# Gate and up with the weights stationary and two token tiles moving, and VectorE's 32x32 turns around the quantisations

## The chip, the core and the metric

The kernel runs on one core of one Trainium2 chip. The metric is the device time of one execution in microseconds. Before the change it is 4258.46 us, the median of three runs (4257.51 to 4258.61). Engine names: TensorE (PE, with its weight loads PEld), VectorE (DVE), ScalarE (ACT), GpSimd (POOL) and SyncE (SP, which issues the DMAs here).

## The reference

One transformer block on x of 8 x 1024 x 512, all in float32. The normed x goes into a causal attention of 16 heads and into a gated network whose linear layers are quantised to a four-bit grid in blocks of 16 along the contracted dimension. Cut to what matters:

```python
def fp4_quant_dequant(x):                       # blocks of 16 along the last dim
    xb = x.reshape(shape[:-1] + (shape[-1] // 16, 16))
    scale = maximum(max(abs(xb), -1, keepdims=True) / 6.0, 1e-12)
    xn = xb / scale
    return (_GRID[searchsorted(_MID, abs(xn))] * sign(xn) * scale).reshape(shape)

def fp4_linear(x, w):                           # w is (n, k)
    return einsum('bsk,nk->bsn', fp4_quant_dequant(x), fp4_quant_dequant(w))

xn = layernorm(x)
h = silu(fp4_linear(xn, w_gate)) * fp4_linear(xn, w_up)      # 512 -> 1408
out = x + attention(xn) + fp4_linear(h, w_down)              # 1408 -> 512
```

## The kernel before

The 8192 tokens are 64 tiles of 128. Attention runs in 64 units (8 batches, 8 pairs of heads). The work is written as generators, and `merge` (L1010) interleaves them into one order of instructions per engine. Each step says its cost on TensorE, the earliest time at which its inputs are there, and how many PSUM banks it needs. A model of time (`clock`, with `act`, `dve` and `pool` for the other engines, L145 to L161) decides which stream goes next, and `Later` (L163) puts an action off to a due time. That order is fixed when the program is built: each engine runs its own queue in order, SP's too.

The streams, each with a place per tile: `weigh` (the softmax weights and their product with the values, L682), `maxima` (row maxima and sums, L557), `networks` (the gated network, L785), `quantised` (x for the network, L438), `preparations` (norm, transpose, projections to q, k and v, 16 tiles ahead, L412) and `finish` (the output projection and the sum, L914).

PSUM has eight banks here: six in a shared set (`Banks`, L187), one accumulator `acc` for the down product, and one, `y`, for the attention. `take` hands out the bank that comes free first, and `back` says when.

The network's way for one tile of 128 tokens:

- `normed` (L392) norms the tokens in `xt`; its `apply` writes them to `xn_kept` in HBM (L408). `quantised` reads them back into `xs` (L442), quantises them on VectorE (`Quantised`, L267, whose operations are L335 to L344) and has TensorE transpose them (`transposed`, L347: four transposes into a bank at L351, one ScalarE copy at L352) into `xqT`.
- `product` (L824) computes gate, later up, for a chunk of 512, 512 or 384 hidden features: `xqT` is the stationary operand, 128 features by 128 tokens, and the weights `wgT` or `wuT` move (L831). The result lies in a bank with tokens on the partitions.
- `gated` (L841) applies SiLU on ScalarE into `hid`, `hidden` (L847) multiplies by up on VectorE, and `Quantised` quantises `hid` in place along its columns, which are the features.
- `turn` (L788) has TensorE transpose the quantised `hid` into a bank, and ScalarE copies it to `hqT`; `down` (L794) multiplies `hqT` by `wdT` (L809) into `acc`. After the last chunk VectorE adds the residual (L815), and the sum goes to `part_kept` in HBM.

Chunks are taken in pairs (L861): both gate products, the down product of the first older chunk, both up products with the transposes of the older second chunk between, its down product, and then the transposes of this pair's first chunk. At most two quantisations run at once; a third forces the rest of the first one out at once (L280).

`project` (L453) computes q and k in another form: the weights `wa` are stationary and two tiles, 256 tokens of `xnT`, move (L466).

Of the kernel before, what the change touches and what calls it, by code (L numbers as in the profile page):

```python
# [27 lines left out]
def kernel(  # L28
# [61 lines left out]
    CW = 4 * P  # L90
    chunks = [(c, min(CW, I - c)) for c in range(0, I, CW)]

# [94 lines left out]
    class Banks:  # L187


        def __init__(self):  # L190
            self.tiles = [ps_g.tile([P, W], F32, name=f"bank{k}") for k in range(6)]
            self.at = [0.0] * 6
            self.held = set()
# [73 lines left out]
    class Quantised:  # L267
# [10 lines left out]

        def __init__(self, src, w, xs, after=0.0):
            while len(running) > 1:  # L280
                running[0].done()
            running.append(self)
            self.out, self.end = xs, 0.0
            self.left = []
            start = max(0.0, after - clock[0])
            for wide, us, engine, action in self.operations(src, w, xs):
                us = us + wide * w / CW
                self.left.append(Later(start, lambda us=us, engine=engine, action=action: self.one(us, engine, action)))
                start += SPREAD * us
            self.expected = clock[0] + start  # L290
# [66 lines left out]
    def weights_quantised():  # L357
# [7 lines left out]
        def load(src, dst, r, c, w):  # L365
            raw = p3.tile([P, CW], F32, name="hid")[:, :w]
            nc.sync.dma_start(out=raw, in_=src[r : r + P, c : c + w])
            return raw
# [23 lines left out]
    def normed(tl):  # L392

        xt = tl.xt
        stats = p4.tile([P, 6], F32, name="stats")
        mv = p4.tile([P, 2], F32, name="mv")
        rstd = p4.tile([P, 1], F32, name="rstd")
        nc.vector.bn_stats(stats, xt)
        nc.vector.bn_aggr(mv, stats)
        nc.vector.tensor_scalar_add(rstd, mv[:, 1:2], EPS)  # L400
        nc.gpsimd.tensor_tensor(rstd, rstd, power, ALU.pow)
        end = pool(0.6, dve(1.1))

        def apply():
            nc.vector.tensor_scalar(xt, xt, mv[:, 0:1], rstd, ALU.subtract, ALU.mult)
            tl.ready = dve(0.57)
            tl.xn = dram.tile([P, D], F32, name="xn_kept", bufs=AHEAD + LAG + 4)
            tl.kept = Later(tl.ready - clock[0] + 0.5, lambda: nc.sync.dma_start(out=tl.xn, in_=xt))  # L408

        tl.applied = Later(end - clock[0] + HOP, apply)  # L410

    def prepare(n):  # L412
# [6 lines left out]
        for i, tl in enumerate(pair):  # L419
            while tl.applied is None:  # L420
                yield 0.0, clock[0] + 0.5, 0
            tl.applied.now()
            yield 0.0, tl.ready, 1
            end = transposed(xnT[:, :, i * P : (i + 1) * P], tl.xt, NC)
            yield 0.45, 0.0, 0
            tl.kept.now()
        for i, tl in enumerate(tiles[n + QT : n + 2 * QT]):
# [9 lines left out]

    def quantised(tl):  # L438

        tl.kept.now()  # L440
        xs = p1.tile([P, CW], F32, name="xs")
        nc.sync.dma_start(out=xs, in_=tl.xn)  # L442
        yield 0.0, clock[0] + 5.0, 0
        xq = Quantised(xs, D, xs)
        yield from xq.wait()
        xqT = p3.tile([P, NC, P], F32, name="xqT")
        tl.there = transposed(xqT, xq.done(), NC)
        tl.xqT = xqT
        yield 0.45, 0.0, 0

# [333 lines left out]

    def network(tiles):  # L785
        emptied = [0.0]

        def turn(job):  # L788
            yield from job.hq.wait()
            job.hqT = p2.tile([P, CW // P, P], F32, name="hqT")  # L790
            job.turned = transposed(job.hqT[:, : job.w // P, :], job.hq.done(), job.w // P)
            yield 0.11 * job.w / P, 0.0, 0

        def down(job):  # L794
            tl = job.tl
            yield 0.0, max(job.turned, emptied[0] if job.i0 == 0 else 0.0), 0
            if job.i0 == 0:
                tl.acc = ps_a.tile([P, D], F32, name="acc")
                tl.xr = p3.tile([P, D], F32, name="res")
                nc.sync.dma_start(out=tl.xr, in_=x[tl.b, tl.t * P : (tl.t + 1) * P, :])  # L800

                def with_bias():
                    nc.gpsimd.tensor_tensor(tl.xr, tl.xr, bp, ALU.add)
                    pool(1.35)

                tl.biased = Later(6.0, with_bias)
            for j in range(job.w // P):
                i = job.i0 // P + j
                nc.tensor.matmul(  # L809
                    tl.acc, lhsT=job.hqT[:, j, :], rhs=wdT[:, i, :], start=(i == 0), stop=(i == NI - 1)  # L810
                )
                if i == NI - 1:
                    xr = tl.xr
                    tl.biased.now()
                    nc.vector.tensor_tensor(xr, tl.acc, xr, ALU.add)  # L815
                    emptied[0] = dve(0.7, clock[0] + 0.86)
                    tl.part = dram.tile([P, D], F32, name="part_kept", bufs=NT + 10)
                    tl.stored = Later(
                        emptied[0] - clock[0] + 1.0, lambda: nc.sync.dma_start(out=tl.part, in_=xr)
                    )  # L820
                if j % 2 == 1 or j == job.w // P - 1:
                    yield 0.86 * (j % 2 + 1), 0.0, 0

        def product(job, wT):  # L824
            while job.tl.xqT is None:
                yield 0.0, clock[0] + 1.0, 0
            yield 0.0, job.tl.there, 1
            job.bank, g = banks.take()
            job.g = g[:, : job.w]
            for c in range(NC):  # L830
                nc.tensor.matmul(  # L831
                    job.g,
                    lhsT=job.tl.xqT[:, c, :],
                    rhs=wT[:, c, job.i0 : job.i0 + job.w],
                    start=(c == 0),
                    stop=(c == NC - 1),
                )
                if c == 1:
                    yield 1.72 * job.w / CW, 0.0, 0

        def gated(job):  # L841
            job.hid = p3.tile([P, CW], F32, name="hid")[:, : job.w]
            nc.scalar.activation(job.hid, job.g, AF.Silu)  # L843
            job.gated = act(job.w, clock[0] + 1.72 * job.w / CW, "silu")
            banks.back(job.bank, job.gated)

        def hidden(job):  # L847
            nc.vector.tensor_tensor(job.hid, job.hid, job.g, ALU.mult)  # L848
            end = dve(0.7, max(job.gated, clock[0] + 1.72 * job.w / CW))
            banks.back(job.bank, end)  # L850
            job.hq = Quantised(job.hid, job.w, job.hid, end)

        def jobs():
            for tl in tiles:
                for i0, w in chunks:
                    yield Job(tl, i0, w)

        stream = jobs()
        older = []
        while True:  # L860
# [3 lines left out]
            for job in pair:  # L864
                yield from product(job, wgT)
                if job is pair[-1]:
                    for each in pair:
                        gated(each)
                yield 1.72 * job.w / CW, 0.0, 0
            if older:  # L870
                yield from down(older[0])
            for k, job in enumerate(pair):
                yield from product(job, wuT)
                hidden(job)
                yield 1.72 * job.w / CW, 0.0, 0
                if k == 0 and older[1:]:
                    yield from turn(older[1])
            if older[1:]:
                if not pair:
                    yield from turn(older[1])  # L880
                yield from down(older[1])
            if pair:
                yield from turn(pair[0])
            older = pair
# [3 lines left out]
    def fetch(tl):  # L888
# [8 lines left out]
        else:  # L897
            parts = [p1.tile([P, NC, P], F32, name=f"yT{part}") for part in range(2)]
            inv = p1.tile([P, NC, P], F32, name="inv_y")
            part = p3.tile([P, D], F32, name="res")  # L900
        for k, yT in enumerate(parts):
# [60 lines left out]
    class Job:  # L962
        def __init__(self, tl, i0, w):
            self.tl, self.i0, self.w = tl, i0, w

    class Tile:
        def __init__(self, n):
            self.n, self.b, self.t = n, n // NT, n % NT
            self.part, self.stored, self.xqT, self.applied, self.fetched = None, None, None, None, None

# [81 lines left out]
    EARLY = PIECES - 6  # L1052
    tiles = [Tile(n) for n in range(N)]
    units = [Unit(n) for n in range(N)]
    batches = []
    units_begun = [-1]

    with tc.manual_schedule(
# [40 lines left out]
        load_values(units[0])  # L1099
        net = network(tiles)  # L1100
        TILE = sum(4 * 1.72 * w / CW + w / P * 0.97 for _, w in chunks)

# [27 lines left out]
        def preparations():  # L1130
            for n in range(AHEAD, N, QT):
# [7 lines left out]
                Stream(networks()),  # L1139
                Stream((quantised(tl), 0.45, tl.n + LAG - 1, 0.5) for tl in tiles),  # L1140
                Stream(preparations()),
# [41 lines left out]
```

## Time and profile before

| What | Value |
|---|---|
| median of three runs | 4258.46 us |
| span of the profiled execution, first to last instruction | 4249.7 us |
| TensorE busy | 4131.2 us (97%), 17684 instructions |
| its weight loads busy | 2619.1 us (62%) |
| VectorE, ScalarE, GpSimd busy | 2763.2 (65%), 2321.8 (55%), 546.5 us (13%) |
| DMA | 573.84 MB, mean 135 GB/s |
| gate and up on TensorE (L831) | 676.1 and 662.9 us busy, 1536 instructions each |
| down (L809) | 665.4 us busy, 1408 instructions |
| transposes (L351) | 836 of hid, 256 of xs, 256 of xt |
| copies of transposed tiles on ScalarE (L352) | 199.0 us busy |
| VectorE in 0 to 500, 2000 to 2500, 3600 to 3900 us | 356.0, 316.9, 209.0 us |

The profiled execution's own time is its span and what lies around it; the median is 8.8 us above the span. Busy time is the union of an engine's instructions. Matmuls overlap in a pipeline and their ends are modelled, so TensorE's busy share is not a measure of its rate. In the waits view each row names who waited, for whom, the sum, how often and the longest.

### The profile page before, as it was taken

How to read it: one execution, taken by the hardware profiler on the slowest of the kernel's cores; microseconds unless marked ns; L12 is line 12 of the kernel's file. 1: busy time of each engine (PE TensorE's matmuls, PEld its weight loads, DVE VectorE, ACT ScalarE, POOL GpSimd, SP SyncE). 2: the span in 40 equal slices, each digit the busy share in tenths (PEclk: the TensorE clock that was granted, in tenths of full speed). 3: DMA queues.
4: the chain of work that ended last, by engine and by line, in shares of the span. 5: the costliest groups of instructions: out<-in, count | busy, mean ns of one | idle time of the engine just before them, and what ended most of it. 6: DMA issues, size and time to landing. Idle time of an engine off the chain costs nothing.

```text
span 4249.7 us, 58555 instructions
## 1 busy us (share of the span) xinstructions
PE 4131.2 (97%) x17684; PEld 2619.1 (62%) x17684; DVE 2763.2 (65%) x7323; ACT 2321.8 (55%) x5918; POOL 546.5 (13%) x1296
## 2 busy tenths in 40 slices
PE   7789999999999999999999999999999999999998
PEld 6666666666666666666666666666666555555555
DVE  6786765666575666575666575666565666667755
ACT  2246556565555565555565555565555666666640
POOL 0001111111111111111111111111111111111110
PEclk9889999999999999999999999999999999999999
DMA  5654434455455455455455455455454433333314
GB/s 183 177 173 129 124 103 120 118 157 157 132 155 150 140 164 153 132 156 151 140 160 155 134 154 149 141 162 153 138 149 131 117 92 94 95 92 93 93 56 126
DMA packets 564187, 573.84 MB, mean 135 GB/s; under 512 B 114976, under 2 KB 420128, under 8 KB 563872
## 3 DMA queue, kind: packets, MB, share of 16 engines
q1 hardware_dynamic: 563872, 570.10, 48.3%
q8 instruction: 142, 2.33, 0.2%
q14 instruction: 173, 1.42, 0.1%
HBM read 400.56 MB, written 169.35 MB: 134 GB/s over the span
## 4 chain that ended last, share of the span: by engine, by line
PE 82%; ACT 7%; DVE 4%; DMA 1%; issue 1%; SPq 0%; ACTq 0%; POOL 0%; DVEq 0%
PE bank L831 26%; PE acc L809 12%; PE bank L466 8%; PE y L706 7%; PE bank L724 6%; PE bank L727 6%; PE bank L597 5%; PE bank L936 5%; PE bank L511 4%; ACT bank L568 3%; PE bank L351 2%; ACT L568 1%; ACT L843 1%; ACT pr L735 1%; DMA ks<-y_kept 1%
## 5 line engine op out<-in xcount | busy, mean ns | idle before, releaser
L568 ACT ACTIVATE bank<-bank,neg 128x512 f32<-128x512 f32 (+3 forms) x1536 | 856.7, 559 | 163.7 <-DVE neg L610 119.8
L735 ACT ACTIVATE pr<-bank 128x512 f32<-128x512 f32 (+3 forms) x1536 | 662.7, 494 | 482.6 <-PE bank L727 478.2
L741 POOL TENSOR_SCALAR_AFFINE_SELECT pr<-pr 128x128 f32<-128x128 f32 x1024 | 393.2, 397 | 3238.3 <-ACT pr L735 3228.9
L610 DVE CUSTOM_DVE_ANT_0 bank<-bank,mask 128x128 f32<-128x128 f32 (+3 forms) x1024 | 501.2, 500 | 469.5 <-PE bank L597 455.7
L724 PE MATMUL bank<-shT,pick 128*128 128x512 f32 (+3 forms) x1536 | 683.8, 453 | 2.7 <-DVE hid L848 1.5
L831 PE MATMUL bank<-wuT,xqT 128*128 128x512 f32 (+1 forms) x1536 | 676.1, 565 | 3.9 <-ACT bank L568 1.0
L809 PE MATMUL acc<-wdT,hqT 128*128 128x512 f32 x1408 | 665.4, 596 | 1.3 <-ACT hqT L352 1.3
L831 PE MATMUL bank<-wgT,xqT 128*128 128x512 f32 (+1 forms) x1536 | 662.9, 561 | 0.0
L597 PE MATMUL bank<-ks,qs 128*128 128x512 f32 (+3 forms) x1536 | 636.2, 475 | 24.7 <-ACT bank L568 21.7
L727 PE MATMUL bank<-qs,ks 128*128 128x512 f32 (+3 forms) x1536 | 516.9, 346 | 0.0
L622 DVE TENSOR_REDUCE neg<-bank 128x1 f32<-128x512 f32 x512 | 345.7, 685 | 186.8 <-PE bank L597 185.6
L597 PEld LDWEIGHTS bank<-ks,qs 128*128 128x128 f32 x1536 | 277.5, 191 | 234.1 <-issue 111.3
L831 PEld LDWEIGHTS bank<-wuT,xqT 128*128 128x128 f32 x1536 | 277.0, 190 | 228.8 <-issue 158.9
L831 PEld LDWEIGHTS bank<-wgT,xqT 128*128 128x128 f32 x1536 | 280.0, 190 | 219.3 <-issue 151.9
L724 PEld LDWEIGHTS bank<-shT,pick 128*128 128x128 f32 x1536 | 290.4, 189 | 155.7 <-issue 78.9
L809 PEld LDWEIGHTS acc<-wdT,hqT 128*128 128x128 f32 x1408 | 255.3, 190 | 197.0 <-issue 183.6
L478 ACT ACTIVATE full<-bank,bqk 128x256 f32<-128x256 f32 x256 | 107.4, 470 | 491.1 <-PE bank L466 409.3
L727 PEld LDWEIGHTS bank<-qs,ks 128*128 128x128 f32 x1536 | 290.6, 189 | 110.6 <-issue 77.1
L466 PE MATMUL bank<-xnT,wa 128*128 128x256 f32 x1536 | 349.8, 381 | 0.9 <-ACT xnT L352 0.6
L466 PEld LDWEIGHTS bank<-xnT,wa 128*128 128x128 f32 x1536 | 288.4, 190 | 55.6 <-issue 18.9
L706 PE MATMUL y<-pr,vs 128*32 128x512 f32 (+3 forms) x3072 | 316.5, 501 | 0.8 <-POOL pr L741 0.8
L568 ACT ACTIVATION_READ_ACCUMULATOR bank<-bank,neg 128x1 f32 x1536 | 315.4, 205 | 0.0
(99 smaller groups left out, 4674.7 us busy)
## 6 DMA issues: line engine op xcount, KB each, us to landing
wa<-in_L_attn_W_attn_dram SPq DMA_DIRECT2D x146, 512.0 KB
qs<-qk_kept SPq DMA_DIRECT2D x512, 128.0 KB
ks<-qk_kept SPq DMA_DIRECT2D x512, 128.0 KB
wp<-in_L_attn_W_proj_dram SPq DMA_DIRECT2D x81, 512.0 KB
qk_kept<-high SPq DMA_DIRECT2D x128, 256.0 KB
qk_kept<-full SPq DMA_DIRECT2D x128, 256.0 KB
y_kept<-yu SPq DMA_DIRECT2D x256, 128.0 KB
yT<-y_kept SPq DMA_DIRECT2D x112, 256.0 KB
```

Of the source, the lines that this page charges most:

```text
L466: nc.tensor.matmul(pq[:, j, :], lhsT=halves[j][:, c, :], rhs=xnT[:, c, :], start=(c == 0), stop=(c == NC - 1),)
L568: nc.scalar.activation(part, part, AF.Exp, bias=neg[:, kind, k + j : k + j + 1], scale=1.0 if kind == 1 else -1.0, accum_out=sums[:, kind, ...
L597: nc.tensor.matmul(sc[:, j * n : (j + 1) * n], lhsT=un.qs[Q][:, r, i * P : (i + 1) * P], rhs=un.ks[h][:, r, :n], start=True, stop=True,)
L610: nc.vector.tensor_tensor_reduce(part, part, mask[:, W - n :], scale=-1.0, scalar=3e38, op0=ALU.add, op1=ALU.min, accum_out=neg[:, kind, k ...
L622: nc.vector.tensor_reduce(neg[:, kind, k : k + 1], sc[:, :n], AX.X, ALU.max, negate=True)
L706: nc.tensor.matmul(y[row : row + HD, q0:], lhsT=un.vs[h][:, jj, r * HD : (r + 1) * HD], rhs=pr[:, q0:], start=(j < 2), stop=(j >= last - 1 ...
L724: nc.tensor.matmul(w[:, q0:], lhsT=pick[:, Q * HU + r, :], rhs=un.shT[:, q0:], start=True, stop=False)
L727: nc.tensor.matmul(w[:, q0:], lhsT=un.ks[h][:, r, jj * P : (jj + 1) * P], rhs=un.qs[Q][:, r, q0:], start=False, stop=True,)
L735: nc.scalar.activation(pr[:, q0:], w[:, q0:], AF.Exp)
L741: nc.gpsimd.affine_select(out=pr[:, q0 : q0 + P], in_=pr[:, q0 : q0 + P], compare_op=ALU.is_ge, fill=0.0, base=0, pattern=[[1, P]], channe ...
L809: nc.tensor.matmul(tl.acc, lhsT=job.hqT[:, j, :], rhs=wdT[:, i, :], start=(i == 0), stop=(i == NI - 1))
L831: nc.tensor.matmul(job.g, lhsT=job.tl.xqT[:, c, :], rhs=wT[:, c, job.i0 : job.i0 + job.w], start=(c == 0), stop=(c == NC - 1),)
```

## The change

Two token tiles are now one twin, and the network works on twins. In `product` the weights are stationary, 128 features of them at a time, and the twin's 256 tokens move. A bank holds two blocks of 128 features by 256 tokens, so gate and up come out with the features on the partitions, as the down product wants its stationary operand. A job is two such blocks, or the last one alone (1408 is 11 x 128).

The quantisation needs the 16 features of a block along a row. `Quantised` with `turned=True` therefore begins and ends with an in-place VectorE transpose, which turns each 32x32 block by itself: between the two, 32 features of a token lie along a row. With that `turn`, its transposes, the copies to `hqT` and the tile `hqT` are gone. For x, `prepare` stores the transposed `xnT` of both tiles to HBM once, and `quantised` loads it for a twin and quantises its two halves in the same turned way, with no transpose on TensorE and no copy. The weights of the network are still quantised and transposed as before.

A twin has two accumulators, `acc0` and `acc1`, so the shared set has five banks. `hid` has four buffers (three before), `xqT` two (of twice the size), `res` two, with a `part` of its own for `finish`. The residual is loaded half-way through a twin's down products.

```diff
-            self.tiles = [ps_g.tile([P, W], F32, name=f"bank{k}") for k in range(6)]
-            self.at = [0.0] * 6
+            self.tiles = [ps_g.tile([P, W], F32, name=f"bank{k}") for k in range(5)]
+            self.at = [0.0] * 5
...
-        def __init__(self, src, w, xs, after=0.0):
+        def __init__(self, src, w, xs, after=0.0, turned=False):
...
-            for wide, us, engine, action in self.operations(src, w, xs):
+            turn = [(0.69, 0.0, "dve", lambda: nc.vector.transpose(out=xs, in_=xs))] if turned else []
+            for wide, us, engine, action in turn + self.operations(src, w, xs) + turn:
...
-            raw = p3.tile([P, CW], F32, name="hid")[:, :w]
+            raw = p4.tile([P, CW], F32, name="hid")[:, :w]
...
-            tl.xn = dram.tile([P, D], F32, name="xn_kept", bufs=AHEAD + LAG + 4)
-            tl.kept = Later(tl.ready - clock[0] + 0.5, lambda: nc.sync.dma_start(out=tl.xn, in_=xt))
...
+        twin = twins[n // QT]
+        twin.xnT = dram.tile([P, NC, QW], F32, name="xn_kept", bufs=(AHEAD + LAG) // QT + 3)
+        twin.kept = Later(end - clock[0] + 0.5, lambda: nc.sync.dma_start(out=twin.xnT, in_=xnT))
...
+    def quantised(twin):
...
+        xqT = p2.tile([P, NC, QW], F32, name="xqT")
+        nc.sync.dma_start(out=xqT, in_=twin.xnT)
+        yield 0.0, clock[0] + 5.0, 0, 0.1
+        halves = [xqT[:, c : c + NC // 2, :].rearrange("p c t -> p (c t)") for c in (0, NC // 2)]
+        working = [Quantised(half, NC // 2 * QW, half, turned=True) for half in halves]
+        for one in working:
+            yield from one.wait()
+            one.done()
+            yield 0.0, 0.0, 0, 0.4
...
-        def turn(job):
-            yield from job.hq.wait()
-            job.hqT = p2.tile([P, CW // P, P], F32, name="hqT")
-            job.turned = transposed(job.hqT[:, : job.w // P, :], job.hq.done(), job.w // P)
-            yield 0.11 * job.w / P, 0.0, 0
...
         def down(job):
+            twin = job.twin
             yield from job.hq.wait()
+            hqT = job.hq.done().rearrange("p (j t) -> p j t", t=QW)
+            if job.first == 0:
+                twin.accs = [ps_a.tile([P, D], F32, name=f"acc{i}") for i in range(QT)]
+            yield 0.0, max(job.hq.end, emptied[0] if job.first == 0 else 0.0), 0
+            for j in range(job.count):
+                n = job.first + j
...
+                for i, tl in enumerate(twin.tiles):
+                    nc.tensor.matmul(
+                        twin.accs[i],
+                        lhsT=hqT[:, j, i * P : (i + 1) * P],
+                        rhs=wdT[:, n, :],
...
         def product(job, wT):
...
-            for c in range(NC):
-                nc.tensor.matmul(
-                    job.g,
-                    lhsT=job.tl.xqT[:, c, :],
-                    rhs=wT[:, c, job.i0 : job.i0 + job.w],
...
+            for j in range(job.count):
+                n = job.first + j
+                for c in range(NC):
+                    nc.tensor.matmul(
+                        job.g[:, j * QW : (j + 1) * QW],
+                        lhsT=wT[:, c, n * P : (n + 1) * P],
+                        rhs=job.twin.xqT[:, c, :],
...
-            for k, job in enumerate(pair):
+            for job in pair:
                 yield from product(job, wuT)
                 hidden(job)
-                yield 1.72 * job.w / CW, 0.0, 0
-                if k == 0 and older[1:]:
-                    yield from turn(older[1])
+                yield 1.72, 0.0, 0
             if older[1:]:
-                if not pair:
-                    yield from turn(older[1])
                 yield from down(older[1])
-            if pair:
-                yield from turn(pair[0])
...
-        TILE = sum(4 * 1.72 * w / CW + w / P * 0.97 for _, w in chunks)
+        TILE = NI * (4 * 1.72 * P / CW * 1.0 + 0.86)
...
-                Stream((quantised(tl), 0.45, tl.n + LAG - 1, 0.5) for tl in tiles),
+                Stream((quantised(twin), 1.0, twin.tiles[0].n + LAG - 1, 0.7) for twin in twins),
```

## The prediction, made before the result was known

> **What bounds the kernel now.** I read four views: the page, the busy time by stretches, TensorE's waits, and TensorE's timeline. First the page and three stretches of 500, 500 and 300 us (columns: length, busy time and instructions of TensorE, its weight loads, VectorE, ScalarE and GpSimd, granted clock, DMA share, GB/s).
>
> ```profile
> span 4249.7 us, 58555 instructions
> PE 4131.2 (97%) x17684; PEld 2619.1 (62%) x17684; DVE 2763.2 (65%) x7323; ACT 2321.8 (55%) x5918; POOL 546.5 (13%) x1296
> ```
>
> ```profile
> 0.00:500.00 500.00, 421.91 (x1906) 315.12 (x1907) 356.01 (x909) 217.95 (x568) 42.97 (x114) 0.93 0.54 157
> 2000.00:2500.00 500.00, 498.05 (x2136) 315.26 (x2134) 316.93 (x851) 284.22 (x723) 66.14 (x155) 1.00 0.54 151
> 3600.00:3900.00 300.00, 295.46 (x1226) 173.64 (x1225) 209.04 (x558) 190.56 (x484) 42.39 (x105) 0.99 0.39 99
> ```
>
> TensorE is idle for 78 us of the first 500 and then for about 2 us in 500; its clock is granted in full. VectorE works 63% in the middle and 70% near the end. Next, all that TensorE waited for from 500 to 4100 us, in total, times, longest:
>
> ```profile
> PE bank L597 <- ACT bank L568: 14.4, 43, 1.1
> PE bank L724 <- DVE hid L848: 1.5, 8, 0.2
> PE bank L831 <- ACT bank L568: 0.7, 3, 0.3
> ```
>
> That is 16.6 us in 3600. A busy engine may still hide waits, since the ends of matmuls are modelled, so I take the rate from the timeline: a group's end minus the end of the group before it.
>
> ```profile
> 2013.59 1.98 PE L831 MATMUL bank<-wuT,xqT 128*128 128x512 f32 x4
> 2015.41 1.04 PE L351 MATMUL bank<-ident,xt 128*128 128x128 f32 x8
> 2016.28 1.88 PE L831 MATMUL bank<-wuT,xqT 128*128 128x512 f32 x4
> ...
> 2019.51 1.99 PE L831 MATMUL bank<-wuT,xqT 128*128 128x512 f32 x4
> 2021.33 3.62 PE L466 MATMUL bank<-xnT,wa 128*128 128x256 f32 x16
> ```
>
> Eight transposes end at 2016.45, the group before at 2015.57: 0.88/8 = 0.110 us each. The next four 512-wide instructions end at 2018.16: 1.71/4 = 0.4275 us. L466, 256 wide, ends at 2024.95 after 2021.50: 3.45/16 = 0.2156 us. (A float32 matmul is two such instructions, a transpose is one.) So from 500 us on the time is the sum of what TensorE streams. What leaves TensorE comes off the end almost one to one, as long as others deliver.
>
> **The change, term by term, against the profiled execution's span of 4249.7 us.** The median of the runs shown, 4258.46, lies 8.8 us above it; I carry the difference of the sum to the median.
>
> *Transposes taken from TensorE.* L351 counts 836 for hid, of which 33 weight pieces keep 11x4 + 11x4 + 4x11 = 132, so 704 go. The 256 for xs go too; the 256 for xt stay. 960 x 0.110 = **-105.6**.
>
> *Waits at the transposes.* Past 500 us the timeline shows them only in the drained end: 0.98, 1.53, 0.93 and 2.06 us before L351, 0.73 and 0.61 before L809, 6.8 in all. The chain up to L344 stays and gets two turns in place of a transpose and a ScalarE copy, so about as much will be late; the 1.53 for xs goes, since a twin is quantised earlier. Bounds -6.8 and +6.8, taken at **-2**.
>
> *Gate and up, the stationary and moving sides swapped.* Columns streamed are equal, pieces smaller. Before: per tile and product, 16 instructions of 512 and 8 of 384. The group of 16 at 4127.61 for 7.03 us, after one that ended at 4127.78, gives 6.86; the 8 of 384 at 4164.41 for 2.74, after 4164.58, give 2.57; together 9.43 x 128 = 1207.0. After: 11 blocks x 4 x 2 = 88 instructions of 256 per twin and product, 88 x 64 = 5632 x 0.2156 = 1214.3. **+7.3**. Weight loads rise from 3072 to 5632 in number. What hides them is the matmul in flight: L466 already pairs each 256-wide instruction with its own load.
>
> ```profile
> L466 PEld LDWEIGHTS bank<-xnT,wa 128*128 128x128 f32 x1536 | 288.4, 190 | 55.6 <-issue 18.9
> ```
>
> A load of 190 ns lies inside 216 ns. With no cover, each would add up to 190 ns, 5632 x 0.19 = 1070 us; L466, same engine, sizes and type, excludes that. [...]
>
> *VectorE's turns.* Per twin, five jobs of 512 columns and one of 256, two turns each, and two halves of x with two turns each: 32 x (10 + 4) = 448 of 512 columns, 64 of 256. The trace has no such turn. One source from SBUF through a simple operation takes 0.425 us (L325), two sources or a reduction 0.68 to 0.70:
>
> ```profile
> L343 DVE TENSOR_TENSOR hid<-hid,step 128x512 f32<-128x512 f32 x158 | 110.2, 701 | 1.9
> L325 DVE TENSOR_SCALAR step<-hid 128x512 int32<-128x512 int32 x158 | 67.2, 425 | 2.8
> ```
>
> Bounds: 0.425, and two such passes of 0.70, 1.40. I take 0.69, because nearly every 512-wide row but the simplest is there, and 0.41 for 256 (L941): 448 x 0.69 + 64 x 0.41 = 335 us. VectorE goes from 2763 to 3098, 74% of the new span. Near the end (3600 to 3900) L809 counts 124, at 22 per tile 5.64 tiles: 53.2 us per tile, 37.1 of VectorE. With 335/64 = 5.2 more in some 51.6 us that is 82%. It fits, but maxima's reductions (L610, L622) stand in the same queue. [...]
>
> *Five banks for six, two accumulators.* A pair of jobs holds two banks through its gate products; three are left for attention instead of four. A tile takes 24 (weigh) + 20 (maxima) + 6 (project) + 6 (products) + 2 (finish) + 2 = 60 banks; in 64 tiles 3840. Below, 0, as now only 43 waits were for banks; above, one exp and its readout (0.669 + 0.205 = 0.87 us) for one taking in 25, +134. VectorE's fuller queue ends in the same waits, because banks come back through it. For both together I let the 16.6 us double, nearest to the row: **+17**.
>
> *Costed at nothing.* 192 ScalarE copies into hqT and xqT (75.0 + 37.6 + 31.5 = 144 us of L352) go; ScalarE is at 55% and hides either way. The store of xn and its reload fall from 64 issues each to 32 of twice the size: 64 issues at about 0.48 us less on SP. New waits: the load of xqT waits on SP for products of two twins earlier, with loads of qs, ks and wa behind it; it is planned a slot after those end, so nothing. The first turn waits on VectorE for 512 KB where L335 waited for 256 KB (idle 0.0 now), with maxima's reductions behind; 2 us late in each of 32 twins would be +64. L809 waits for the last turn instead of L352, with every other stream behind it on TensorE; the chain is begun a whole product phase earlier. Four hid buffers instead of three may save part of the 14.5 us that VectorE waits for weights: -14.5 to 0, taken at 0, since preparation runs beside it.
>
> Sum: -105.6 - 2 + 7.3 + 17 = -83.3; the span becomes 4166, the median **4175**.
>
> **Rivals.** *All waits stay as small as now*: without the 17, with every lower bound, -105.6 - 6.8 - 14.5 = -127, 4132. *The stand-ins eat most of it*: xqT late by 2 us per twin, +64, on top of the forecast: 4239. For it speaks a DMA share of 0.5 in the middle; against it, that L335 never waited. *Five banks decide (slower)*: L597 and L724 wait for banks while two are held by the gate pair. The point is (105.6 + 2 - 7.3)/3840 = 26 ns per taking; one exp in 25 takings costs 134, so 4258 - 100 + 134 = 4292. For it speaks that all but 1.5 of the 16.6 us are bank waits; against, that products and down need no new bank for long stretches and fill. *A turn costs 1.40*: VectorE adds 678 us, near the end 37.1 + 10.6 = 47.7 of 51.6 us, 92%; with 3 us of waiting in each of the 20 tiles from 3400 on and 1 us in the other 44, +104: about 4262, no change. *The change doesn't do what it says*: weight loads of 190 ns not hidden at 256 would show as L831 well over 0.2156; even 26 ns more, 5632 x 0.026 = 146, gives 4321. L466 speaks against it.
>
> **How the numbers follow.** Forecast with its small-wait rival, 4132 to 4215: 0.60. Most of it eaten, 4215 to 4250: 0.14. About no change, mostly the turn at 1.40: 0.07. Slower, the banks (0.15) or loads not hidden (0.04): 0.19. The measurement can tell 0.2% from no change, 8.5 us, so faster 0.74, same 0.07, slower 0.19. The range goes from 4132 to 4295, past the bank rival's 4292; about 0.15 is left out.
>
> **What would show it.** L351 falls from 1348 to 388; L831 has 5632 instructions ending 0.2156 us apart; turns near 0.69 us; VectorE about 74%; L352 without hqT and xqT; the waits from 500 to 4100 us near 33 us. I am wrong if L597 or L724 waits for banks by over 100 us, if a turn is over 1 us, or if the stretches past 500 us show TensorE idle by some per cent.

## The result and the profile after

The changed kernel takes 4563.35 us (median of four runs, 4554.60 to 4563.61) against 4257.99 for the kernel before: a ratio of 1.0714, 95% interval 1.0701 to 1.0727. The prediction was 4175 us, with a range from 4132 to 4295. The profiled execution spans 4552.9 us; its own time is 4554.60.

The page, and the same stretches as shown of before (length, busy time and instructions of TensorE, weight loads, VectorE, ScalarE, GpSimd, clock, DMA share, GB/s):

```profile
span 4552.9 us, 61768 instructions
PE 4181.5 (92%) x19284; PEld 3049.1 (67%) x19284; DVE 3087.0 (68%) x7835; ACT 2208.8 (49%) x5662; POOL 509.0 (11%) x1296
```

```profile
0.00:500.00 500.00, 423.50 (x1954) 331.74 (x1954) 362.86 (x909) 206.01 (x526) 40.52 (x112) 0.91 0.52 153
2000.00:2500.00 500.00, 459.39 (x2117) 337.43 (x2116) 325.29 (x836) 246.90 (x634) 53.71 (x140) 0.96 0.48 134
3600.00:3900.00 300.00, 288.48 (x1324) 201.22 (x1323) 221.48 (x560) 164.57 (x421) 41.58 (x104) 0.97 0.36 94
```

The start is unchanged. In the middle TensorE is now idle 41 us in 500 instead of 2, and its clock is granted at 0.96. What it waits for from 500 to 4100 us (total, times, longest):

```profile
PE bank L729 <- ACT pr L740: 178.1, 18, 10.4
PE bank L844 <- ACT bank L573: 21.2, 39, 0.9
PE bank L602 <- ACT bank L573: 20.9, 72, 1.6
PE bank L660 <- DVE stat L656: 15.1, 6, 2.9
PE bank L602 <- ACT full L483: 13.3, 19, 0.7
```

One wait of about 10 us comes 18 times; from 988 to 3383 us the timeline has it every 140 us, once per twin. (Lines have moved: L724 is now L729, L597 L602, L831 L844, L809 L806.) What ScalarE waits for, and SP's second longest wait, tell why:

```profile
ACT yu L774 <- DMA y_kept<-yu: 291.3, 18, 16.7
```

```profile
SPq L502 <- DVE high L496: 507.5, 123, 13.6
```

Before, ScalarE never waited for that store, and SP's wait for the split was 284.8 us in 118:

```profile
SPq L497 <- DVE high L491: 284.8, 118, 8.4
```

Here is one such moment in the timelines of VectorE, SP, ScalarE and TensorE, in this order (start, length, instruction, idle time before and its releaser):

```profile
1951.13 1.26 DVE L285 STREAM_TRANSPOSE xqT<-xqT 128x512 f32<-128x512 f32 x2
...
1964.29 0.71 DVE L285 STREAM_TRANSPOSE xqT<-xqT 128x512 f32<-128x512 f32 x1
1964.92 0.39 DVE L496 CAST high<-full 128x512 fp32r<-128x512 f32 x1
```

```profile
1951.37 0.40 SPq L234 DMA_DIRECT2D wa<-in_L_attn_W_attn_dram  x1
1965.34 0.37 SPq L502 DMA_DIRECT2D qk_kept<-high  x1
...
1971.42 1.10 SPq L780 DMA_DIRECT2D y_kept<-yu  x2
```

```profile
1951.38 0.84 ACT L483 ACTIVATE full<-bank,bqk 128x256 f32<-128x256 f32 x2 [3.23 <-PE bank L471]
1952.91 0.59 ACT L774 COPY yu<-y 128x512 f32<-128x512 f32 x1 [0.69 <-PE y L711]
...
1975.51 0.59 ACT L774 COPY yu<-y 128x512 f32<-128x512 f32 x1 [15.97 <-DMA y_kept<-yu]
```

```profile
1965.07 1.89 PE L844 MATMUL bank<-xqT,wgT 128*128 128x256 f32 x8
1976.64 0.80 PE L729 MATMUL bank<-shT,pick 128*128 128x512 f32 x1 [9.68 <-ACT pr L740]
```

Read it from the top. VectorE does both halves of a twin's x from 1951 to 1965. The split of a q and k projection (L496), whose input ScalarE finished at 1952.2, stands behind them until 1964.9. SP has been waiting for it since 1951.8. Behind it on SP stand ten loads and then the store of `yu`, which leaves at 1971.4. `yu` has one buffer, so ScalarE's next copy waits until 1975.5, and the exps behind it, which give back the banks, wait too. TensorE runs out of banks at 1967. Four queues in order, TensorE's, VectorE's and ScalarE's at 92, 68 and 49% by the page, pass one late instruction on.

The pause has an echo. In three stretches from it on (same columns as above) the granted clock is 0.70, 0.51 and 1.00:

```profile
1965.00:1977.00 12.00, 2.32 (x10) 1.72 (x10) 9.01 (x18) 1.50 (x3) 0.00 (x0) 0.70 0.91 224
1977.00:1980.00 3.00, 3.00 (x6) 1.80 (x6) 0.00 (x0) 2.95 (x5) 0.00 (x0) 0.51 0.98 268
1980.00:1985.00 5.00, 5.00 (x18) 3.19 (x17) 0.76 (x2) 2.21 (x5) 2.50 (x2) 1.00 0.25 92
```

After this pause the half clock lasts some 3 us, after others up to 6. Around the 18 pauses TensorE is busy for 73 us at half the clock, which loses some 36 us; this is an estimate, half of that time. But the pauses are not all. The trace's clock record has 20 more stretches at half the clock from 500 us on, with 100 us of TensorE's busy time in them, and none of these belongs to one of the 18 pauses. That makes 172 us busy at half the clock and a loss of some 86 us by the same estimate; in the kernel before it is 7 us and a loss of 3. The mean granted clock of the whole span falls from 0.991 to 0.958. In the pause shown TensorE stands from 1967.0 to 1976.6; the clock record has half the clock from 1969.7 to 1979.9, so it begins 2.7 us into the pause and ends 3.3 us after TensorE starts again. What sets off the stretches outside the pauses isn't shown.

### The profile page after: what moved, and what is told of

The parts are those of the page before. It is cut to its first block, busy times and chain, and to the rows that moved or that the text cites. A ratio compares the mean times of both kernels' runs of the same rounds, so it can differ in the third digit from the quotient of the medians.

```text
span 4552.9 us, 61768 instructions
## 1 busy us (share of the span) xinstructions
PE 4181.5 (92%) x19284; PEld 3049.1 (67%) x19284; DVE 3087.0 (68%) x7835; ACT 2208.8 (49%) x5662; POOL 509.0 (11%) x1296
## 4 chain that ended last, share of the span: by engine, by line
PE 67%; DVE 13%; ACT 7%; issue 4%; DMA 3%; SPq 2%; ACTq 0%; DVEq 0%
PE bank L844 24%; PE acc L806 10%; PE bank L729 5%; PE y L711 5%; PE bank L732 5%; PE bank L471 5%; PE bank L943 4%; PE bank L602 4%; PE bank L516 4%; ACT bank L573 3%; DMA y_kept<-yu 1%; DVE bank L615 1%; ACT pr L740 1%; SPq L545 1%; DVE scale L335 1%
## 5 line engine op out<-in xcount | busy, mean ns | idle before, releaser
L729 PE MATMUL bank<-shT,pick 128*128 128x512 f32 (+3 forms) x1536 | 658.2, 437 | 180.4 <-ACT pr L740 178.1
L844 PE MATMUL bank<-xqT,wuT 128*128 128x256 f32 x2816 | 687.6, 388 | 7.7 <-ACT bank L573 3.1
L806 PE MATMUL acc<-wdT,hid 128*128 128x512 f32 x1408 | 686.0, 614 | 5.5 <-DVE hid L285 5.5
L844 PE MATMUL bank<-xqT,wgT 128*128 128x256 f32 x2816 | 665.1, 384 | 22.7 <-ACT bank L573 21.0
L746 POOL TENSOR_SCALAR_AFFINE_SELECT pr<-pr 128x128 f32<-128x128 f32 x1024 | 366.1, 371 | 2806.0 <-ACT pr L740 2795.1
L602 PE MATMUL bank<-ks,qs 128*128 128x512 f32 (+3 forms) x1536 | 585.3, 450 | 52.7 <-ACT bank L573 29.3
L844 PEld LDWEIGHTS bank<-xqT,wgT 128*128 128x128 f32 x2816 | 528.6, 191 | 119.0 <-ACT bank L573 32.1
L844 PEld LDWEIGHTS bank<-xqT,wuT 128*128 128x128 f32 x2816 | 528.7, 193 | 110.6 <-ACT bank L573 14.2
L732 PE MATMUL bank<-qs,ks 128*128 128x512 f32 (+3 forms) x1536 | 524.6, 352 | 0.0
L729 PEld LDWEIGHTS bank<-shT,pick 128*128 128x128 f32 x1536 | 294.6, 192 | 307.2 <-ACT pr L740 193.1
L602 PEld LDWEIGHTS bank<-ks,qs 128*128 128x128 f32 x1536 | 282.6, 197 | 236.0 <-ACT bank L573 103.8
L806 PEld LDWEIGHTS acc<-wdT,hid 128*128 128x128 f32 x1408 | 272.5, 199 | 219.4 <-issue 200.8
L732 PEld LDWEIGHTS bank<-qs,ks 128*128 128x128 f32 x1536 | 296.0, 193 | 60.6 <-issue 32.1
L774 ACT COPY yu<-y 128x512 f32<-128x512 f32 x128 | 75.2, 587 | 497.9 <-DMA y_kept<-yu 291.3
```

Of the source, the lines that this page charges most:

```text
L602: nc.tensor.matmul(sc[:, j * n : (j + 1) * n], lhsT=un.qs[Q][:, r, i * P : (i + 1) * P], rhs=un.ks[h][:, r, :n], start=True, stop=True,)
L729: nc.tensor.matmul(w[:, q0:], lhsT=pick[:, Q * HU + r, :], rhs=un.shT[:, q0:], start=True, stop=False)
L732: nc.tensor.matmul(w[:, q0:], lhsT=un.ks[h][:, r, jj * P : (jj + 1) * P], rhs=un.qs[Q][:, r, q0:], start=False, stop=True,)
L746: nc.gpsimd.affine_select(out=pr[:, q0 : q0 + P], in_=pr[:, q0 : q0 + P], compare_op=ALU.is_ge, fill=0.0, base=0, pattern=[[1, P]], channe ...
L806: nc.tensor.matmul(twin.accs[i], lhsT=hqT[:, j, i * P : (i + 1) * P], rhs=wdT[:, n, :], start=(n == 0), stop=(n == NI - 1),)
L844: nc.tensor.matmul(job.g[:, j * QW : (j + 1) * QW], lhsT=wT[:, c, n * P : (n + 1) * P], rhs=job.twin.xqT[:, c, :], start=(c == 0), stop=(c ...
```

## The experiments

Theory A: the chain just read. Theory B: five banks instead of six. Theory C: VectorE has too much to do with the turns. Theory D joined later: the order that `merge` makes of its constants. Each ratio is to the kernel before on the same chip.

**The halves one after the other.**

```diff
-        working = [Quantised(half, NC // 2 * QW, half, turned=True) for half in halves]
-        for one in working:
+        working = []
+        for half in halves:
+            one = Quantised(half, NC // 2 * QW, half, turned=True)
+            working.append(one)
             yield from one.wait()
```

> The changed kernel, but the second half of a twin's x starts its quantisation only when the first is done; all the work stays. Theory A (a chain of queues: once per twin VectorE gets both halves at once, the split of the q and k projections L496 stands some 12 us behind them, SP waits for it with the stores of yu behind, ScalarE waits for its only yu buffer, TensorE for a bank): the split waits some 6 us less, the 178 us of L729 behind ScalarE fall below 60, the time from 4563 to 4340 to 4460 us. Theory B (five banks instead of six): no change, 4563 within 30. Theory C (VectorE has too much to do with the turns, 74% of the span): no change, 4563 within 30.

4469.13 us, 1.0499 (1.0484 to 1.0515). The chain is gone: ScalarE has no wait for the store of `yu`. But the time fell by 94 only, just outside what A had said, since x of a twin is ready later and the order becomes another: from 1960 to 1975 us blocks of maxima run with almost nothing between, and they wait for banks, 119.7 us over the whole run where it was 29.3 (L602 is L604 here).

```profile
PE bank L604 <- ACT bank L575: 119.7, 168, 5.3
```

The clock takes its part too: from 500 us on TensorE is busy for 241 us at half the clock, a loss of some 120 us by estimate, where the changed kernel has 86.

**The stores of yu issued by ScalarE.**

```diff
-                    nc.sync.dma_start(
+                    nc.scalar.dma_start(
                         out=un.batch.y[part, f, rows, Q * W : (Q + 1) * W],
```

> The changed kernel, but the 256 stores of yu are issued from ScalarE's queue instead of SP's, so they no longer stand behind SP's wait for the split. Theory A: ScalarE no longer waits 16 us for the store (291 us in all for L774), L729's 178 us go, and with them the slow clock behind each; about -178 - 45 = -220, 4340 us within 50, though ScalarE pays 256 issues of about 0.5 us. Theory B: no change or slower, 4563 to 4600. Theory C: no change or slower, 4563 to 4600.

4346.00 us, 1.0207 (1.0190 to 1.0224): 217 us less, with the order of instructions untouched; besides cutting the link, the edit only moves the issuing of 256 stores from SP to ScalarE. The 178 us are gone, and what TensorE waits for longest past 500 us is now

```profile
PE bank L844 <- ACT bank L573: 23.7, 44, 0.9
PE bank L660 <- DVE stat L656: 19.6, 8, 2.9
```

A is right, with its size: 178 us of pauses, and some 36 us of slow clock (from 500 us on 101 us busy at half the clock are left, a loss of some 51 by estimate instead of 86). 4346 is still 171 us above the prediction, so A isn't all.

**The kernel before with five banks.**

```diff
-            self.tiles = [ps_g.tile([P, W], F32, name=f"bank{k}") for k in range(6)]
-            self.at = [0.0] * 6
+            self.tiles = [ps_g.tile([P, W], F32, name=f"bank{k}") for k in range(5)]
+            self.at = [0.0] * 5
```

> The kernel before, with five shared banks instead of six and nothing else. Theory A: the banks cost little, 4258 to 4300 us. Theory B: most of the loss shows here, 4400 to 4560 us. Theory C: 4258 to 4300 us.

4394.79 us, 1.0324 (1.0308 to 1.0339). The bank, with the order that `merge` makes for five, costs 138 us here, less than B had said and far more than A had allowed. In the waits past 500 us:

```profile
PE bank L597 <- ACT bank L568: 47.5, 95, 1.5
PE bank L831 <- ACT pr L735: 8.5, 34, 0.5
PE bank L831 <- ACT bank L568: 4.8, 27, 0.2
```

These rows hold some 61 us, 44 more than before. The rest does not show as idle time. Part of it is the clock: from 500 us on TensorE is busy for 78 us at half the clock, a loss of some 39 us by estimate, against 3 before. For what is left I have an argument and no measurement: the weight load of a group that waits for a bank waits as well, and a product that was ready in the middle of the stream follows late. The waits of weight loads for ScalarE were the row that I hadn't read. Here it is over the whole run, in the kernel before and in this one; in the changed kernel it is 103.8 us.

```profile
PEld bank L597 <- ACT bank L568: 73.2, 169, 2.9
PEld bank L597 <- ACT bank L568: 140.7, 273, 2.8
```

**No turns planned.** The tuple `turn` is left out, so the blocks lie along the tokens; that part of the computation is left out.

```diff
-            for wide, us, engine, action in turn + self.operations(src, w, xs) + turn:
+            for wide, us, engine, action in self.operations(src, w, xs):
```

> The changed kernel without the 512 turns on VectorE (338 us of its time); the blocks are then quantised along the tokens, so this part of the computation is left out. Theory A: the two halves still come at once, 10 us instead of 12, so the wait shrinks only in part: 4430 to 4530 us. Theory B: little change, 4500 to 4563 us. Theory C: VectorE is back at its old load, about 4180 to 4260 us.

4333.28 us, 1.0178 (1.0163 to 1.0193). Below what A and B had said and above C's. But the planner knows of the missing turns and makes another order, in which the chain doesn't occur. The run can't tell load from order, which led to the ninth and tenth.

**Six banks for the changed kernel.** Both tiles of a twin accumulate into one bank, so that the sums of the two tiles are not kept apart; matmuls, turns and DMAs are all there.

```diff
-            self.tiles = [ps_g.tile([P, W], F32, name=f"bank{k}") for k in range(5)]
+            self.tiles = [ps_g.tile([P, W], F32, name=f"bank{k}") for k in range(6)]
...
-                twin.accs = [ps_a.tile([P, D], F32, name=f"acc{i}") for i in range(QT)]
+                twin.accs = [ps_a.tile([P, D], F32, name="acc")] * QT
...
-                        start=(n == 0),
-                        stop=(n == NI - 1),
+                        start=(n == 0 and i == 0),
+                        stop=(n == NI - 1 and i == QT - 1),
...
```

> The changed kernel with six shared banks again: both tiles of a twin accumulate into one bank, so the sums of the two tiles are not kept apart and this part of the computation is changed; all matmuls, turns and DMAs stay, yu still goes through SP. Theory A (the chain from VectorE's queue over SP and ScalarE costs some 217 us and needs no bank shortage): ScalarE still waits for yu, 4400 to 4460 us. Theory B (the missing bank is the root, the chain only its result): the waits behind ScalarE go too, 4170 to 4260 us.

4275.40 us, 1.0036 (1.0023 to 1.0049). The wait for `yu` is gone without touching SP. It was gone with five banks too in the first and the fourth run, whose orders differ from the changed kernel's, so the chain belongs to an order, not to the change as such. 15 us above B's range.

**The same with the stores of yu issued by ScalarE.** The edit of the fifth, and with it that of the second:

```diff
-                    nc.sync.dma_start(
+                    nc.scalar.dma_start(
```

> As the run with six banks and one accumulator (the two tiles' sums are not kept apart), and the stores of yu from ScalarE's queue. Theory A and B together (chain 217, bank about 137, gain of the transposes about 100): 4346 - 137 = 4209, between 4170 and 4250 us, below the kernel before. If the bank's cost in the kernel before was only an unlucky order: above 4290.

4279.01 us, 1.0045 (1.0030 to 1.0060). Where there is no chain, moving the stores gains nothing. The sum of A and B (4209) fails by 70: with six banks and no chain the gain still doesn't show. In both runs blocks of maxima still come in a lump once per twin, in the fifth at 1889 to 1899 us for instance, with half a clock after it: the eight 256-wide matmuls of L845 that end at 1902.29, after a group that ended at 1898.64, are 0.456 us apart instead of 0.215. That is about the size of what is missing: from 500 us on TensorE is busy for 157 us (fifth) and 150 us (sixth) at half the clock, a loss of some 79 and 75 us by estimate, against 3 in the kernel before.

**Other constants of the merge.** On top of the second experiment; the last line is the number of blocks of maxima held.

```diff
-    SOONER = 0.3
-    QUEUE = 2.0
-    SURE = 0.4
-    AHEAD_OF_OTHERS = 0.6
-            while len(older) > 3:
+    SOONER = 0.4
+    QUEUE = 1.5
+    SURE = 0.3
+    AHEAD_OF_OTHERS = 0.7
+            while len(older) > 2:
```

> The changed kernel with yu stored by ScalarE and other constants of the merge (SOONER 0.4, QUEUE 1.5, SURE 0.3, AHEAD_OF_OTHERS 0.7, two blocks of maxima held instead of three): the same work and banks in another order. Theory B (five banks cost about 137 in any order): 4320 to 4370 us. Theory D (much of the loss is the order that came out of these constants): 4240 to 4300 us.

4260.58 us, 1.0003 (0.9993 to 1.0012): 85 us less than the second experiment with the same work, the same five banks and no chain in either. D.

**The kernel before with other constants.**

```diff
-    SOONER = 0.3
-    QUEUE = 2.0
-    LATE = 0.6
-    SURE = 0.4
-    AHEAD_OF_OTHERS = 0.6
-            while len(older) > 3:
+    SOONER = 0.4
+    QUEUE = 1.0
+    LATE = 0.3
+    SURE = 0.2
+    AHEAD_OF_OTHERS = 0.7
+            while len(older) > 2:
```

> The kernel before with other constants of the merge (SOONER 0.4, QUEUE 1.0, LATE 0.3, SURE 0.2, AHEAD_OF_OTHERS 0.7, two blocks of maxima held): the same work in another order. Theory B: TensorE streams without a pause already, so nothing is left to win, 4245 to 4275 us. Theory D: the order matters by itself, 4180 to 4240 us or above 4300.

4218.72 us, 0.9903 (0.9888 to 0.9917). The kernel before wasn't at its end either; this is the fastest whole version of this study, faster than both kernels.

**The turns left out, the order kept.** The planner is told of them, VectorE doesn't get them (that part of the computation is left out).

```diff
-            turn = [(0.69, 0.0, "dve", lambda: nc.vector.transpose(out=xs, in_=xs))] if turned else []
+            turn = [(0.69, 0.0, "dve", lambda: None)] if turned else []
```

> The changed kernel in exactly its own order, with the 512 turns left out of VectorE's queue (this part of the computation is left out), yu through SP. Theory A (the chain starts in VectorE's queue): the split waits 12 us less four to six turns, 3 to 4 us, so most of ScalarE's wait for yu (291 us) goes or halves; 4340 to 4460 us. Theory D (the order alone sets it, VectorE's work does not matter): 4530 to 4563 us.

4480.16 us, 1.0525 (1.0508 to 1.0543): 83 us less. The pauses are still 18, and shorter, and so is SP's wait for the split (507.5 us before this edit):

```profile
PE bank L729 <- ACT pr L740: 115.3, 18, 8.1
SPq L502 <- DVE high L496: 396.9, 123, 9.9
```

That is A's first link: VectorE's queue is shorter by the turns, and the pause shrinks with it. It also shows that the turns are not the root, because both halves at once suffice for it. The time is 20 us above A's range, and ScalarE's wait for `yu` fell from 291 to 232 us only, not to half.

**The turns left out, the order kept, and the stores of yu issued by ScalarE.** The last edit and that of the second experiment together (the turns are left out here too).

> As the run without turns in the same order, with yu stored from ScalarE's queue: against 4346 us with the turns it tells what VectorE's 338 us cost beside the chain. Theory C (VectorE's load): 4200 to 4270 us. Theories B and D (banks, order): 4310 to 4350 us.

4354.65 us, 1.0224 (1.0209 to 1.0240), against 4346.00 with the turns. With the chain cut, 308 us less on VectorE (2776.5 busy, where the second experiment has 3084.5) gain nothing. C falls.

**Five banks in the better order of the kernel before** (the constants of the eighth, five banks).

```diff
-            self.tiles = [ps_g.tile([P, W], F32, name=f"bank{k}") for k in range(6)]
-            self.at = [0.0] * 6
+            self.tiles = [ps_g.tile([P, W], F32, name=f"bank{k}") for k in range(5)]
+            self.at = [0.0] * 5
```

> The kernel before in the better order's constants (4219 us with six banks), with five banks. Theory B (a bank less costs about 137 us in any order): 4330 to 4380 us. Theory D (that cost was one unlucky order): 4210 to 4260 us.

4292.91 us, 1.0084 (1.0069 to 1.0099): 74 us over the same constants with six banks. Between B and D: a bank less costs something in both orders, 138 and 74, and how much is a matter of the order.

**The changed kernel whole, in another order**.

```diff
-    QUEUE = 2.0
-    LATE = 0.6
-    SURE = 0.4
-    SPREAD = 1.4
-    AHEAD_OF_OTHERS = 0.6
-            while len(older) > 3:
+    QUEUE = 1.5
+    LATE = 0.8
+    SURE = 0.3
+    SPREAD = 1.5
+    AHEAD_OF_OTHERS = 0.7
+            while len(older) > 1:
```

> The changed kernel, whole and with yu through SP, in another order: QUEUE 1.5, LATE 0.8, SURE 0.3, SPREAD 1.5, AHEAD_OF_OTHERS 0.7, one block of maxima held instead of three. Theory D (the loss lies in the order, the chain and the bank waits with it): 4170 to 4230 us, below the kernel before by up to the transposes' 100. Theory B (five banks cost what they cost): 4300 us or more. Theory A alone, if the chain comes back in this order: above 4350 us.

4292.96 us, 1.0082 (1.0067 to 1.0097): 270 us less than the changed kernel by constants alone, yet short of D's range. The long pause of L729 is down from 178.1 to 15.8 us in all; new are waits at single places, 13.3 us for the statistics at 3352 us.

**All three together:** one accumulator and six banks (the sums not kept apart), `yu` stored by ScalarE, and another order. Beside the edits of the sixth:

```diff
-    SOONER = 0.3
-    LATE = 0.6
-    SURE = 0.4
-    SPREAD = 1.4
-    AHEAD_OF_OTHERS = 0.6
-            while len(older) > 3:
+    SOONER = 0.35
+    LATE = 0.5
+    SURE = 0.5
+    SPREAD = 1.6
+    AHEAD_OF_OTHERS = 0.7
+            while len(older) > 1:
```

> The changed kernel with six banks and one accumulator (the sums of a twin's two tiles are not kept apart), yu stored by ScalarE, in another order: SOONER 0.35, LATE 0.5, SURE 0.5, SPREAD 1.6, AHEAD_OF_OTHERS 0.7, one block of maxima held. With neither the chain nor the missing bank, what the order leaves decides. If the transposes' 100 us are really free on TensorE and only the waits of the order hid them: 4110 to 4190 us, well below the 4219 of the kernel before in its better order less at least 30. If the smaller matmuls or VectorE's turns eat them in any order: 4215 us or more.

4138.48 us, 0.9717 (0.9701 to 0.9734). The page and the middle stretch of this run:

```profile
PE 4014.4 (97%) x19284; PEld 3002.8 (73%) x19284; DVE 3034.6 (73%) x7835; ACT 2211.3 (53%) x5662; POOL 500.9 (12%) x1296
```

```profile
2000.00:2500.00 500.00, 499.93 (x2421) 375.40 (x2421) 364.92 (x953) 279.44 (x716) 62.20 (x163) 1.00 0.56 156
```

All matmuls and turns of the change are in it, and TensorE is never idle in the middle. In this order what was taken from TensorE does come off the end. Its busy time is 98 us below the 4112.5 of the eighth run, as much as the prediction had (105.6 less 7.3), so the smaller matmuls and the turns eat little of it. From 500 us on it is busy at half the clock for 36 us, in the eighth run for 26.

## Why the prediction was wrong

The direction was wrong. Its terms, one by one:

- *The engines' work was right.* L351 fell from 1348 to 388. A turn takes 706 ns (hid) and 687 (xqT) at 512 columns and 423 at 256, where 0.69 and 0.41 were taken. VectorE is busy 3087 us, 3098 were worked out. The 256-wide matmuls run at 0.215 us: a group of eight at 1943.35 for 1.89, after one that ended at 1943.52, is 1.72/8. Their 5632 weight loads, 191 and 193 ns each by the rows of L844, are hidden: with a load for every matmul, the matmuls still end 0.215 us apart. One count was wrong without effect: the copies that went are 256 (192 into hqT, 64 into xqT).
- *That the gain comes off the end was right in principle*: the thirteenth run is 119 us below the kernel before and 80 below its better order, around the predicted 100. The orders differ in both comparisons, so neither number is the gain itself.
- *"For both together I let the 16.6 us double, nearest to the row: +17" is the step that failed.* The rows shown of 500 to 4100 us sum to 249 us instead of 33, 178 of them the chain's pauses. One reason is that the term was sized by the waits of an order that the change replaces. The order is made anew from the banks and costs of all streams, and its quality is no property of the edit: constants alone moved the changed kernel by 85 us (second to seventh) and 270 (whole kernel to twelfth), the kernel before by 41. The other is that the bank wasn't worth a few waits but 138 or 74 us. VectorE's fuller queue, the other half of the term, cost nothing beside the chain (tenth run). The bank rival had this mechanism, with 134 us and a chance of 0.15: by itself the right sign, but 4292 and not 4563. That the third run's 138 lies so near its 134 is luck, since the same bank costs 74 in the other order and the rival's takings were miscounted: `project` takes six banks for two tiles, so a tile takes 57 and not 60, which makes 127 us.
- *The slow clock is in no term*: the prediction read "granted in full" and carried it over. From 500 us on the changed kernel loses some 86 us to it by estimate, the kernel before 3.
- *"The first turn waits on VectorE ... with maxima's reductions behind" named the wrong instruction behind.* The load was not late (VectorE is idle for 1.6 us in all before the 128 turns of xqT); the burst itself is the delay, and the one that mattered behind it was the split, with SP behind the split, ScalarE behind SP, and TensorE behind ScalarE. On SP I costed the load of xqT and the issues saved, but did not ask what any SP instruction waits for on VectorE. Put at nothing, this step cost 217 us (second experiment).
- *The rival of a late xqT* asked for the right queue, with the wrong cause and a third of the price. *The turn at 1.40* and *weight loads not hidden* did not happen.

The accounts: predicted 4175, measured 4563, 388 us. The chain is 217 of it (second experiment). The other 171 are waits for banks, the slow clock and the order that both come from, together (the second experiment still loses some 51 us to the clock by estimate): another order with five banks gave 85 of them back (4261), six banks with the first constants 67 to 71 (4279, 4275), both with a better order more than all (4138).

What stays open: bank and order can't be told apart further, since a sixth bank always makes another order; so the bank's price is a span, 74 to 138 us in the kernel before. What halves the clock where no long pause stands before it is open too. And whether the change can win as a whole kernel isn't shown: the best with separate sums is 4261 against 4219 for the kernel before in its better order. A version with six banks that keeps the two sums apart was not tried.

## What to carry to other kernels

Before an edit puts a burst on an engine, list what stands behind it in that engine's queue, what SP waits for from those, and what stands behind that on SP: here `yu`, single-buffered at the end of such a chain, held up ScalarE, 49% busy, for 291 us. Where a planner makes the order, an edit of banks or costs draws a new order, worth one to six per cent here; try both versions under several constants before judging the edit. A resource that shows few idle waits may still be the tight one (in the third run a bank less cost 138 us, with 61 us in the rows of TensorE's waits): read the waits of the weight loads and the granted clock too.

## What the hardware showed that was not expected

A pause of 10 us on TensorE is followed by some 3 us at a granted clock of 0.51, in which the 512-wide matmuls of L729 and L732 end 0.43 us apart instead of the 0.23 just before the pause. ScalarE issuing the 256 stores of `yu` itself cost at most some 4 us (4279.01 against 4275.40 us), with ScalarE half busy (53% in the thirteenth run, which has the same edit). The clock was at half not only after pauses: in the kernel before with five banks, where no wait of TensorE from 500 to 4100 us is longer than 1.5 us, it was busy for 78 of the 79 us that the record has at half the clock from 500 us on.
